# TensorE in program order through the main loop of a four-layer convolution and attention kernel, and four steps of a side chain moved

## The chip, the cores and the metric

The kernel runs on one core of one Trainium2 chip. The time is the device time of one execution in microseconds (us). Before the change it is 1875.23 us, the median of three runs (1875.23 to 1875.4).

The engines are named as in the profile: PE is TensorE's matmul, PEld its weight load, DVE is VectorE, ACT is ScalarE, POOL is GpSimd, SP is SyncE, which issues most transfers. A float32 matmul appears as two records, two passes, each with its own weight load.

## What is computed

The input is 8 batches of 512 channels by 32 x 32 positions (N = 1024), all in float32. Four layers follow each other.

```python
# layer 0: attention without softmax, divided by its largest singular value
f = relu(batchnorm(Wf x)); g = relu(batchnorm(Wg x)); h = Wh x      # 64 channels
z = f^T g; x = Wv (h (z / sigma_max(z))^T) + x
# layer 1: group norm, then softmax attention with 512 channels
hn = groupnorm(x); q, k, v = Wq hn, Wk hn, Wv hn
x = x + Wp (softmax(q^T k / sqrt(512)) v)
# layer 2: softmax attention with 128 channels
t, p, g = split(W_w x); x = batchnorm(Z_w (softmax(t^T p / sqrt(128)) g)) + x
# layer 3: a 1x1 convolution of signs
s = bn(scale * (sign(W) sign(x + bias))) + x; out = where(t > 0, t, slope * t) + bias2   # t = s - shift
```

The largest singular value is found by repeated squaring of a small matrix, in a chain of 64 x 64 products per pair of batches (`chain`), with the matrix turned by VectorE between two products.

## The kernel before

The work before the main loop (to about 175 us of the span) does layer 0's projections for all batches, the merged weights of layer 1, and the singular value of the first pair of batches. The main loop then calls `fast(env, n, hb, ua)` for n = 0 to 7, one batch each. One call traces, in this order:

1. `scores1`: layer 1's logits and their exponentials, four groups of seven products (Strassen-like, `seven`, L422). Each of `seven`'s results is copied by ScalarE (`move`, L367) or added by VectorE (`plus`, L373). The matmuls are called by the names of their factors: A11·B11, S1·T1, S2·T2, S4·B22, S3·T3, A12·B21, A22·T4, in that order. A11·B11, S2·T2, S3·T3 and A22·T4 go into one bank of PSUM, S1·T1 and S4·B22 into a second, A12·B21 into a third. Between two of these steps the last half of layer 3 of the batch before (`leave`, held in `rest3`) is traced, and the entry of the next batch: `weights0` (L313) and `enter` (L446, L467, L474), matmuls with 64 rows or a few columns.
2. `make_v` (values of layer 1), with the sums of exponentials (L1033, `inverse_sums`) and their way through memory.
3. `values1` (L751), which ends layer 1. In it the next batch is normalized, and the first two factors for its U are prepared (`prepare_u`, on POOL, L582 to L584, with a load of `fac` by SP).
4. `project2`: layer 2's projections, seven products (L422) and then 8 steps of 4 matmuls (L852).
5. `scores2`: 8 x 2 logits (L1011), each with its exp on ScalarE (L1018); VectorE adds the exponentials (L1005).
6. `values2` (L1172), `inverse_sums` (L1033), `close2` (L871), the first half of layer 3 (`leave`: signs L882 on ScalarE, products L894, then L905, L906, L907, L915, L937, L938, L945 on ScalarE and VectorE).

U of the next batch (`make_u2`) is made in the gaps of stages 4 and 5: a generator of 7 x 4 steps, of which `fill()` takes one after each step of `project2` (15) and after each L1011 (16). One block of four steps is `inner`: seven small products (L606, 128 x 256, 0.43 us each in two passes) into two banks. `p1` holds two of the sums, `pa` in its left half and `pc` in its right half; `p2` holds the third, `pb`.

```python
product(pa, 0, True, False);  move(d11, pa)      # step 0
product(pc, 3, False, False); move(d22, pc)
product(pa, 2, False, False); move(d12, pa)      # step 1
product(pc, 4, False, True);  plus(d12, pc, d12, 0)
product(pa, 5, False, False); plus(d22, pa, d22, 1)   # step 2
product(pb, 1, True, True);   plus(d11, pb, d11, 0)
product(pa, 6, False, True);  move(d21, pa, 1)   # step 3
```

`move` is a copy by ScalarE (L623, or L625 with a bias), `plus` an addition by VectorE (L617, or L619 with a bias). At the end of a block POOL adds finished parts into U by transfers (L658), and the next factors are prepared.

The chain for the singular values of the other pairs of batches runs behind all this: `chore(now)` takes one step of it. In batch 0 there are 23 such places: 10 in `scores1`, 4 in `make_v`, 5 in `values1` and 4 in `project2`. A step is one or two L1239 and perhaps an L1276 on PE, with copies by ScalarE (L1257) or VectorE (L1259, L1261), turns by VectorE (L1246, L1251), sums of a diagonal (L1270), and at a chain's start a power on POOL (L1289). At the end of a chain ScalarE takes a logarithm (L1318) and an exponential (L1321), each with a load of its table, VectorE scales in between (L1319 to L1323).

The order in which each engine gets its instructions is set by a scheduler while the program is built: it goes by a model of times and by priority, so it may take an instruction ahead of one that was traced earlier if that one would still wait. Exceptions are instructions marked with `keep_in_program_order`, and blocks under `manual_schedule`, in which the named engine's instructions keep the order in which they were traced. Before the change the work ahead of the main loop has such a block for PE, and the main loop has none. The scheduler adds all waits that data or a shared bank need.

## Time and profile before

| what | time |
|---|---|
| median of three runs | 1875.23 us |
| profiled execution | 1877.21 us, of which span 1875.3 us |
| PE busy | 1851.4 us |
| DVE busy | 1181.0 us |
| ACT busy | 572.2 us |
| POOL busy | 379.5 us |

The span is the time from the first to the last instruction of the profiled execution; its own time is 1.9 us longer. TensorE's granted clock was 0.998 of full speed.

Batch 1, cut at the first matmuls of its stages (us from the span's start; each row is how long an engine was busy in that stretch):

| stretch | stage | length | PE | DVE | ACT | POOL |
|---|---|---|---|---|---|---|
| 498.2 to 547.1 | `values1` | 48.9 | 48.90 | 39.40 | 3.93 | 20.66 |
| 547.1 to 580.6 | `project2` with U | 33.5 | 33.39 | 18.00 | 8.38 | 13.42 |
| 580.6 to 604.1 | `scores2` with U | 23.5 | 23.50 | 10.57 | 12.72 | 12.37 |
| 604.1 to 616.5 | `values2` | 12.4 | 12.40 | 9.89 | 0.96 | 0.86 |
| 616.5 to 627.6 | `close2` and first half of `leave` | 11.1 | 11.10 | 6.76 | 5.35 | 0.00 |
| 627.6 to 709.9 | next batch's `scores1`, `make_v` | 82.3 | 82.29 | 59.09 | 34.88 | 1.18 |

How to read the profile's lines: a line of the timeline has the start in us, the length in us, the engine, the line of the kernel, the operation, what it writes and reads, the shape and how many instructions are merged into it, and in brackets how long the engine was idle before it and what released it. A line of the waits has the engine and what waited, what it waited for, the total in us, how often, and the longest.

### The profile page before, as it was taken

How to read it: one execution, taken by the hardware profiler on the slowest of the kernel's cores; microseconds unless marked ns; L12 is line 12 of the kernel's file. 1: busy time of each engine (PE TensorE's matmuls, PEld its weight loads, DVE VectorE, ACT ScalarE, POOL GpSimd, SP SyncE). 2: the span in 40 equal slices, each digit the busy share in tenths (PEclk: the TensorE clock that was granted, in tenths of full speed). 3: DMA queues.
4: the chain of work that ended last, by engine and by line, in shares of the span. 5: the costliest groups of instructions: out<-in, count | busy, mean ns of one | idle time of the engine just before them, and what ended most of it. 6: DMA issues, size and time to landing. Idle time of an engine off the chain costs nothing.

```text
span 1875.3 us, 18038 instructions
## 1 busy us (share of the span) xinstructions
PE 1851.4 (99%) x6490; PEld 1004.1 (54%) x6490; DVE 1181.0 (63%) x2188; ACT 572.2 (31%) x1022; POOL 379.5 (20%) x403
## 2 busy tenths in 40 slices
PE   9999999999999999999999999999999999999997
PEld 3365464644646465654646455654646464644653
DVE  3356777567765768567764777467654767366447
ACT  2042221344213521244214522244213521244114
POOL 1002004310224003420224003320234004310011
PEclk9999999999999999999999999999999999999999
DMA  8641000242006210242006210242006200340001
GB/s 280 202 137 46 20 17 1 65 101 89 12 10 128 92 37 1 56 105 85 21 4 125 84 54 1 52 108 80 21 10 128 97 25 1 71 91 23 12 1 47
DMA packets 57532, 119.05 MB, mean 63 GB/s; under 512 B 7200, under 2 KB 17244, under 8 KB 57180
## 3 DMA queue, kind: packets, MB, share of 16 engines
q1 hardware_dynamic: 42844, 91.70, 14.8%
q0 software_dynamic: 13728, 25.70, 8.0%
q8 instruction: 53, 0.87, 0.2%
q10 hardware_dynamic: 864, 0.43, 0.1%
q14 instruction: 43, 0.35, 0.1%
HBM read 68.92 MB, written 23.20 MB: 49 GB/s over the span
## 4 chain that ended last, share of the span: by engine, by line
PE 95%; DVE 3%; ACT 1%; DMA 1%; issue 0%; POOL 0%; DVEq 0%; ACTq 0%
PE bank L422 37%; PE bank L751 21%; PE bank L606 8%; PE bank L1172 6%; PE bank L1011 5%; PE bank L1560 4%; PE bank L871 3%; PE bank L852 3%; PE bank L446 2%; PE bank L894 1%; PE wide L1606 1%; PE bank L1664 1%; PE bank L1239 1%; PE quad L1452 0%; PE bank L1033 0%; DVE st L458 0%
## 5 line engine op out<-in xcount | busy, mean ns | idle before, releaser
L751 PE MATMUL bank<-e,vt 128*128 128x512 f32 x768 | 336.2, 594 | 0.0
L751 PEld LDWEIGHTS bank<-e,vt 128*128 128x128 f32 x768 | 144.3, 190 | 172.3 <-issue 167.2
L422 PE MATMUL bank<-ut,h 128*128 128x512 f32 x384 | 180.7, 597 | 0.0
L244 POOL TENSOR_TENSOR r_r<-r_v,minus_half 128x4 f32<-128x4 f32 (+1 forms) x11 | 11.0, 1001 | 699.6 <-DVE r_v L243 694.2
L1011 PE MATMUL bank<-tpg 128*128 128x512 f32 x256 | 126.6, 592 | 0.0
L606 PE MATMUL bank<-jit,fac 128*128 128x256 f32 x392 | 118.5, 390 | 4.4 <-ACT ut L623 2.4
L422 PEld LDWEIGHTS bank<-ut,h 128*128 128x128 f32 x384 | 71.2, 190 | 90.7 <-issue 79.2
L422 PE MATMUL bank<-us,hs 128*128 128x512 f32 x256 | 118.9, 597 | 0.1
L1172 PE MATMUL bank<-e,tpg 128*128 128x512 f32 x256 | 114.7, 595 | 0.0
L606 PEld LDWEIGHTS bank<-jit,fac 128*128 128x128 f32 x392 | 67.3, 189 | 76.6 <-issue 24.9
L373 DVE TENSOR_TENSOR e<-bank,e 128x512 f32<-128x512 f32 x96 | 65.8, 689 | 61.9 <-PE bank L422 55.8
L1018 ACT ACTIVATE e<-bank 128x512 f32<-128x512 f32 x128 | 76.4, 597 | 87.0 <-PE bank L1011 87.0
L582 POOL TENSOR_TENSOR jit<-h 128x256 f32<-128x256 f32 x56 | 49.5, 905 | 209.7 <-PE bank L606 122.8
L422 PE MATMUL bank<-wo,h 128*128 128x256 f32 x384 | 89.8, 384 | 0.0
L367 ACT COPY e<-bank 128x512 f32<-128x512 f32 x96 | 55.0, 581 | 95.1 <-PE bank L422 88.7
L422 PEld LDWEIGHTS bank<-us,hs 128*128 128x128 f32 x256 | 47.6, 190 | 63.1 <-issue 54.8
L1172 PEld LDWEIGHTS bank<-e,tpg 128*128 128x128 f32 x256 | 48.1, 190 | 57.4 <-issue 56.9
L422 PEld LDWEIGHTS bank<-wo,h 128*128 128x128 f32 x384 | 71.4, 190 | 12.6 <-issue 3.8
L882 ACT ACTIVATE sg<-xt,rb 128x512 f16<-128x512 f32 x64 | 44.2, 717 | 106.5 <-DVE xt L873 103.7
L623 ACT COPY ut<-bank 128x256 f32<-128x256 f32 x126 | 46.9, 372 | 96.2 <-PE bank L606 93.4
L373 DVE TENSOR_TENSOR vt<-bank,vt 128x512 f32<-128x512 f32 x48 | 33.2, 692 | 66.3 <-PE bank L422 65.5
L367 ACT COPY vt<-bank 128x512 f32<-128x512 f32 x64 | 37.4, 584 | 121.3 <-PE bank L422 121.2
(391 smaller groups left out, 3341.0 us busy)
## 6 DMA issues: line engine op xcount, KB each, us to landing
xt<-in_x SPq DMA_DIRECT2D x55, 512.0 KB
fac<-fac_dram SPq DMA_DIRECT2D x49, 448.0 KB
out<-both SPq DMA_DIRECT2D x63, 256.0 KB
ut<-ut POOLq DMA_DIRECT2D x28, 512.0 KB, 5.0
ut<-p POOLq DMA_DIRECT2D x42, 256.0 KB, 4.1
rfull<-r_dram SPq DMA_DIRECT2D x15, 512.0 KB
f_dram<-f SPq DMA_DIRECT2D x8, 256.0 KB
fb<-f_dram SPq DMA_DIRECT2D x8, 256.0 KB
```

What stands on the lines that cost most here:

```text
L367: nc.scalar.copy(dst, ps)
L373: nc.vector.tensor_tensor(dst, ps, u, ALU.add)
L422: mm(out=ps[:, q * w : (q + 1) * w], lhsT=lt(ka, kb, q, k), rhs=rhs(ka, kb, q, k), start=first and q == 0 and k == 0, stop=last and k == 1 ...
L582: tt(t[:, k], b[:, k, hi], b[:, 0, bass.ts(k, QF)], ALU.subtract)
L606: mm(out=out, lhsT=fac[:, blocks[a], :], rhs=rhs[b], start=first, stop=last, skip_group_check=True,)
L751: mm(out=ps, lhsT=a[:, t, bass.ts(r_, P)], rhs=e[t], start=first and t == 0, stop=last and t == NTH - 1, skip_group_check=True,)
L852: mm(out=ps[:, i, :], lhsT=xt[:, cc, bass.ts(4 * h + i, P)], rhs=sbw["tpg"][:, cc, 2 * P : 3 * P], start=cc == 0, stop=cc == CC - 1,)
L871: mm(out=ps, lhsT=sbw["z"][:, bass.ts(oc, P)], rhs=att, start=True, stop=True)
L1011: mm(out=ps, lhsT=pt[:, 0, bass.ts(t, P)], rhs=tt[:, 0, half(h)], start=True, stop=True,)
L1018: nc.scalar.activation(e[:, half(h)], ps, AF.Exp, scale=float(P) ** -0.5)
L1172: mm(out=banks[h], lhsT=gt[:, t, :], rhs=es[t][:, half(h)], start=t == 0, stop=t == NT - 1,)
L1560: mm(out=banks[i][side(h), :], lhsT=w0[i][:, cc, :], rhs=xt[:, cc, half(h)], start=cc == 0, stop=cc == CC - 1,)
```

## The change

The calls of `fast` in the main loop are traced in a `manual_schedule` block for PE. So TensorE's instructions of the main loop stand in the program in the order in which the code traces them; the other engines are still ordered by the scheduler. And in batch 0 (n == 0) the four `chore` steps that were taken in `project2`, after its steps 2, 5, 8 and 12, are taken in `scores2`, after the second half of t = 1, 3, 5 and 7. In the batches after it nothing is moved by hand.

```diff
         for k, _ in enumerate(project2(env, xt, made)):
             fill()
-            chore(k in (2, 5, 8, 12))
+            chore(n and k in (2, 5, 8, 12))
         tt, pt, gt = made
 
         def between(t, h):
             fill()
+            chore(n == 0 and h and t in (1, 3, 5, 7))
 
         es, esum = scores2(env, pt, tt, between)
@@
         ua = got[0]
         late_u = factors_of_u(env)
-        for n in range(B):
-            hb, ua = fast(env, n, hb, ua)
+        with tc.manual_schedule(engines={mybir.EngineType.PE}):
+            for n in range(B):
+                hb, ua = fast(env, n, hb, ua)
```

In the built programs, two parts of TensorE's order in batch 1 (L606 with the number of the product in `inner`):

```
        before                            after
scores2, sixth block of U (and the fifth's last product)
        L1011                             L1011
        L606 5 (fifth block)              L606 6 (fifth block)
        L606 0                            L1011
        L1011                             L606 0
        L606 6 (fifth block)              L606 3
        L606 3                            L1011
        L1011                             L606 2
        L606 2                            L606 4
        L606 1                            L1011
        L1011                             L606 5
        L606 4                            L606 1
from the end of scores2 to the next batch's scores1
        L1011 x2, L606 6, L1172 x3        L606 6, L1011 x3, L1172 x2
        L1033 x4                          L1033 x4
        L1172 x10, L871 x4, L1172 x3      L1172 x10, L871 x4, L1172 x4
        L894 x8, L871 x4                  L894 x8, L871 x4
        A11 B11 x2, S1 T1 x2              A11 B11 x2, S1 T1 x2
        L894, half of A12 B21             S2 T2 x2
        S2 T2 x2                          S4 B22 x2
        L894 x2, half of A12 B21          L894 x4
        S4 B22 x2, L894, S3 T3 x2         S3 T3 x2, A12 B21 x2
        L894 x4, A22 T4 x2                L894 x4, A22 T4 x2
```

Elsewhere in the loop the order differs in the same way in `project2`; in `scores1` of batches 1, 3 and 5 the two L313 stand together after the change and apart before it, in batches 2, 4 and 6 the four L446 of the first visit. In `make_v` and `values1` nothing moves. SP's order is the same, and POOL's differs only in the place of L1289.

## The prediction

> **What bounds the kernel now.** I read the page first: busy shares, then the chain that ended last.

> ```profile
> PE 1851.4 (99%) x6490; PEld 1004.1 (54%) x6490; DVE 1181.0 (63%) x2188; ACT 572.2 (31%) x1022; POOL 379.5 (20%) x403
> ...
> PE 95%; DVE 3%; ACT 1%; DMA 1%; issue 0%; POOL 0%; DVEq 0%; ACTq 0%
> ```

> TensorE (PE) is the bound: it stands still for 1875.3 − 1851.4 = 23.9 us in all, so nothing can be gained beyond that and some packing, while any wait put into its queue is added to the end. The list of waits, for PE alone, has almost nothing on the line that makes U (L606):

> ```profile
> PE bank L606 <- ACT ut L623: 2.4, 2, 2.0
> ```

> The timeline of batch 0 shows why:

> ```profile
> 333.53 0.59 PE L606 MATMUL bank<-h,fac 128*128 128x256 f32 x2
> ...
> 333.96 1.02 PE L422 MATMUL bank<-xd,sp 128*128 128x512 f32 x2
> 334.21 0.38 ACT L623 COPY ut<-bank 128x256 f32<-128x256 f32 x1
> ...
> 334.64 0.37 PEld L606 LDWEIGHTS bank<-jit,fac 128*128 128x128 f32 x2 [0.49 <-ACT ut L623]
> 334.82 0.59 PE L606 MATMUL bank<-jit,fac 128*128 128x256 f32 x2
> ```

> A product of `inner` ends, ScalarE copies it out, and the weights of the next L606 wait for that copy, since `pa` and `pc` are halves of one bank (`p1`). One L422 (0.86 us) lies between and covers it. Timelines at the seam between two batches and at the end of `scores2` come below.

> [...]

> **Part 1: pairs of L606.** `inner` issues products 0,3 | 2,4 | 5,1 | 6. In program order nothing stands inside a step, so 3 follows 0 and 4 follows 2 directly, each waiting for the copy of its partner; 1 goes to another bank and is free. The trace of before has no such pair; its price from parts: from the start of the first product to its last record's end 0.59, to the copy 0.04, the copy 0.37, to the next weight load 0.05, and 0.11 until it streams. That last one is from a stall in the same timeline, where the next matmul comes 0.54 after this one instead of 0.43:

> ```profile
> 349.88 0.70 PE L606 MATMUL bank<-jit,fac 128*128 128x256 f32 x2 [0.47 <-DVE ut L617]
> ...
> 350.42 0.59 PE L606 MATMUL bank<-hs,fac 128*128 128x256 f32 x2
> ```

> That makes 1.16 us instead of 0.43: a stall of 0.73 with ScalarE free. Less is excluded, as every part is needed. Behind L1011 the exp (L1018, 0.60 us, beginning 0.20 after L1011's end) runs until 0.80, so the copy starts 0.17 later: 0.90. More than 0.90 needs another instruction in ScalarE's queue; I take 0.73 and 0.90. Per batch seven blocks of U, two pairs each: in `scores2` 6 pairs at 0.90, in `project2` 2 at 0.90 (behind L367, 0.59 us) and 6 at 0.73. That is 5.4 + 1.8 + 4.4 = 11.6 us, and 7 batches make U (98 such pairs stand in the new order, none in the old): **+81.1**.
> What goes: the present stalls of these two stages, by starts beyond the streaming time: 0.64 + 2.12 + 0.17 + 0.47 = 3.4 in batch 0 and about 1.2 in each of the six later ones (0.83 + 0.42 in batch 4): **−10.6**. Between steps stand L422 x2 (1.72), L852 x4 (0.88) or L1011 (0.86), over the 0.73 needed, so 2 after 3 and 5 after 4 cost nothing as long as ScalarE and VectorE are free.

> **Part 2: the seam between batches.** In the timeline of batch 1:

> ```profile
> 627.64 1.88 PE L422 MATMUL bank<-ut,h 128*128 128x512 f32 x4
> ...
> 629.36 1.88 PE L422 MATMUL bank<-us,hs 128*128 128x512 f32 x4
> ...
> 631.70 0.56 ACT L367 COPY e<-bank 128x512 f32<-128x512 f32 x1
> ...
> 632.32 1.98 PE L422 MATMUL bank<-us,hs 128*128 128x512 f32 x4
> ...
> 634.72 1.05 ACT L367 COPY e<-bank 128x512 f32<-128x512 f32 x2
> ...
> 635.43 1.90 PE L422 MATMUL bank<-us,h 128*128 128x512 f32 x4
> ```

> S2·T2 (632.32) waits for the copy of A11·B11 (ends 632.26), S4·B22 (635.43) for that of S1·T1 (ends 635.25). The copies stand behind L937, L938 and L882 of `leave`. Before, L894s and half of A12·B21 fill the room; in the new order S2·T2 and S4·B22 follow at once, and L1172 x4 instead of x3 stands before the first L894, which moves that ScalarE work 0.86 later. Counted from the first L871 (616.47): S1·T1 ends at 3.43 + 3.43 + 1.72 + 3.43 + 3.43 = 15.45; the copy ends at 15.79 + 0.86, plus 0.16 to the stream, 16.8: stall 1.35. S2·T2 ends at 18.5, the second copy allows 19.8: stall 1.28. Waits of 0.34 here go: net 2.3, seven times: **+16.1**. If the work of `leave` does not move, 1.7 of each goes.

> **Part 3: L1033.** Only two L1172 (1.72 us) precede it, not three:

> ```profile
> 603.24 3.88 DVE L1005 TENSOR_TENSOR esum<-esum,e 128x1024 f32<-128x1024 f32 x3
> ...
> 604.55 2.74 PE L1172 MATMUL bank<-e,tpg 128*128 128x512 f32 x6
> ```

> The sum ends at 607.12, just when the third L1172 does. In the new order exp (0.20 + 0.60) and the last add (1.23) follow the last L1011, with handoffs 2.2 us against 1.72: 0.5 for batches 1 to 6, 0.3 in the last (the same on L1062): 3.3.
> Batch 0 is worse: the four chores, the same instructions (on PE L1239 and L1276, 0.11 us a pass), now end a chain inside `scores2`, where VectorE was busy 14.4 of 28 us. Its two table loads (1.28 each), L1318 and L1321 stand on ScalarE before three of the exps, and on VectorE (DVE) three adds wait for `rsig` and then queue with the next chain's 2.3 us. I count from the start of L1011 for t = 6: exp free at 1.7; rsig 5.1; gm 5.7; two adds 8.2; chain 10.4; last add 11.7, while PE arrives at 6.0: 5.7. Together **+9.0**. In exchange POOL's pow (L1289) no longer stands before `jit` work; what it cost is among the 3.4. DMA issues: SP's order is unchanged, POOL's additions (L658) keep theirs, and later matmuls give them more room.

> **Part 4: packing.** Matmuls of 64 rows run side by side when adjacent:

> ```profile
> 652.32 1.12 PE L446 MATMUL bank<-fb,pv 64*128 64x512 f32 x2
> ...
> 655.29 1.98 PE L446 MATMUL bank<-fb,pv 64*128 64x512 f32 x6
> ```

> One alone holds PE 1.05, three 1.91; four together take 1.92 elsewhere. Three such quads (batches 2, 4, 6) and three split pairs of L313 (batches 1, 3, 5) are whole in the new order: 6 × 1.05 = **−6.3**.

> Sum: 81.1 + 16.1 + 9.0 − 10.6 − 6.3 = **+89.3**. The profiled execution took 1877.2 (span 1875.3 and 1.9 around it), the median 1875.2; the same amount goes on both. Forecast for the median: **1964 us**.

> **Rivals.** (a) Bank waits only: the seam is covered, all pairs cost 0.73: 98 × 0.73 + 9.0 − 16.9 = +64, 1939 us. For: the waits of `leave` are estimates from one batch; against: the copies already end last there. (b) Evictions queue: the gap between steps has some 0.1 us to spare, and an add (1.23) ahead of L617 or an exp ahead of L623 costs another 0.5 per pair: +49, 2013 us. [...] against: with PE slower it is idle half the time. (c) Faster: if a pair's wait cost under 0.17 us and the seam nothing, parts 1 and 4 would win: at 0.1, 9.8 − 16.9, 1868 us. The point is the turnaround PE, ScalarE, PE; the measured parts give 0.73. (d) The new order changes nothing PE notices: 1875; against it the new order itself, in which the pairs are adjacent.

> **How the numbers follow.** Forecast 0.66, with its own range 1948 to 1985; (a) 0.17, (b) 0.12, (c) 0.03, (d) 0.02. The range 1930 to 1995 leaves out (c), (d) and most of (b). A measurement tells about 0.2% (3.8 us) from no change: faster 0.03, same 0.02, slower 0.95.

> **What would show it.** PE's waits list L606 after ACT L623 some 80 to 98 times, 0.6 to 0.8 idle each; L422 after ACT L367 about 1.3 twice per seam; L1033 after DVE L1005 once of some 5 us; L313 and L446 only in full groups. No L606 wait in the list would make the prediction wrong; L606 waiting for DVE would be rival (b).

## The result and the profile after

The changed kernel takes 1960.86 us (median of five runs, 1960.32 to 1961.92); the kernel before, run beside it, 1875.23 us. The ratio is 1.0456 with a 95% interval of 1.0441 to 1.0472: slower by 4.6%, 85.6 us. The profiled execution has a span of 1958.7 us, 83.4 more than the 1875.3 of before.

In the changed kernel the first 1163 lines of the code are where they were; a line after them is one further down (L1172 is L1173 here).

The page of the changed kernel, busy times and instructions by engine:

```profile
PE 1863.8 (95%) x6490; PEld 996.4 (51%) x6490; DVE 1177.3 (60%) x2188; ACT 569.5 (29%) x1022; POOL 378.8 (19%) x403
```

The instructions are the same in number on every engine. TensorE's busy time grew by only 12 us, while 1958.7 − 1863.8 = 94.9 us of the span are now idle, against 23.9 before. No other engine has become the bound: all are at most 60% busy. So the question is only what TensorE waits for. Its list of waits (what waited, for what, us in total, how often, the longest):

```profile
PE bank L606 <- ACT ut L623: 35.8, 70, 0.6
PE bank L422 <- ACT e L367: 16.2, 18, 1.1
PE bank L606 <- ACT p L623: 15.8, 28, 0.6
PE bank L1033 <- DVE esum L1005: 7.1, 7, 5.7
```

Four rows hold 74.9 of the 94.9 us. The first and the third are the pairs of L606: 70 + 28 = 98 waits, 14 in each of the seven batches that make U. The second is the seam between batches. The fourth is one wait of 5.7 us in batch 0 and six of 0.2 to 0.3.

One pair in the timeline of the changed kernel (batch 4, `scores2`; start, length, engine, line, what; in brackets the idle time before and its releaser):

```profile
1270.44 0.59 PE L606 MATMUL bank<-hs,fac 128*128 128x256 f32 x2
...
1270.64 0.60 ACT L1018 ACTIVATE e<-bank 128x512 f32<-128x512 f32 x1 [0.33 <-PE bank L1011]
1271.14 0.37 ACT L623 COPY ut<-bank 128x256 f32<-128x256 f32 x1
...
1271.62 0.30 PEld L606 LDWEIGHTS bank<-jit,fac 128*128 128x128 f32 x2 [0.98 <-POOL jit L582]
1271.65 0.67 PE L606 MATMUL bank<-jit,fac 128*128 128x256 f32 x2 [0.61 <-ACT ut L623]
...
1272.15 1.02 PE L1011 MATMUL bank<-tpg 128*128 128x512 f32 x2
```

Product 0 of a block streams from 1270.44. Its copy L623 waits until the exp L1018 is out of ScalarE's way and runs from 1271.14; product 3 starts only at 1271.65, and the L1011 behind it waits with it. From one L606 to the next are 1.21 us instead of 0.43.

### The profile page after: what moved, and what is told of

Its sections match the earlier page's. It is cut to its first block, busy times and chain, and to the rows that moved or that the text cites. A ratio compares the mean times of both kernels' runs of the same rounds, so it can differ in the third digit from the quotient of the medians.

```text
span 1958.7 us, 18010 instructions
## 1 busy us (share of the span) xinstructions
PE 1863.8 (95%) x6490; PEld 996.4 (51%) x6490; DVE 1177.3 (60%) x2188; ACT 569.5 (29%) x1022; POOL 378.8 (19%) x403
## 5 line engine op out<-in xcount | busy, mean ns | idle before, releaser
L422 PE MATMUL bank<-ut,h 128*128 128x512 f32 x384 | 178.1, 598 | 1.4 <-ACT e L367 1.4
L606 PE MATMUL bank<-jit,fac 128*128 128x256 f32 x392 | 120.8, 390 | 27.4 <-ACT ut L623 18.9
L1011 PE MATMUL bank<-tpg 128*128 128x512 f32 x256 | 126.2, 593 | 0.0
L422 PE MATMUL bank<-us,hs 128*128 128x512 f32 x256 | 117.5, 596 | 7.6 <-ACT e L367 7.6
L422 PEld LDWEIGHTS bank<-ut,h 128*128 128x128 f32 x384 | 70.9, 190 | 95.1 <-issue 84.3
L1173 PE MATMUL bank<-e,tpg 128*128 128x512 f32 x256 | 115.9, 600 | 0.0
L606 PEld LDWEIGHTS bank<-jit,fac 128*128 128x128 f32 x392 | 66.2, 189 | 97.3 <-issue 45.8
L1018 ACT ACTIVATE e<-bank 128x512 f32<-128x512 f32 x128 | 76.2, 597 | 117.1 <-PE bank L1011 117.1
L582 POOL TENSOR_TENSOR jit<-h 128x256 f32<-128x256 f32 x56 | 49.8, 909 | 233.1 <-PE bank L606 146.1
L422 PE MATMUL bank<-wo,h 128*128 128x256 f32 x384 | 89.9, 384 | 0.0
L367 ACT COPY e<-bank 128x512 f32<-128x512 f32 x96 | 55.1, 581 | 102.2 <-PE bank L422 102.2
L422 PEld LDWEIGHTS bank<-us,hs 128*128 128x128 f32 x256 | 47.8, 190 | 69.8 <-issue 56.2
L617 DVE TENSOR_TENSOR ut<-bank,ut 128x256 f32<-128x256 f32 x63 | 26.8, 425 | 89.9 <-PE bank L606 89.8
L1173 PEld LDWEIGHTS bank<-e,tpg 128*128 128x128 f32 x256 | 48.5, 192 | 61.0 <-issue 60.9
L623 ACT COPY ut<-bank 128x256 f32<-128x256 f32 x126 | 46.9, 372 | 108.3 <-PE bank L606 108.3
L422 PEld LDWEIGHTS bank<-wo,h 128*128 128x128 f32 x384 | 71.4, 190 | 12.6 <-issue 3.8
L882 ACT ACTIVATE sg<-xt,rb 128x512 f16<-128x512 f32 x64 | 44.1, 715 | 107.2 <-DVE xt L873 104.4
```

Of the source, the lines that this page charges most:

```text
L367: nc.scalar.copy(dst, ps)
L422: mm(out=ps[:, q * w : (q + 1) * w], lhsT=lt(ka, kb, q, k), rhs=rhs(ka, kb, q, k), start=first and q == 0 and k == 0, stop=last and k == 1 ...
L582: tt(t[:, k], b[:, k, hi], b[:, 0, bass.ts(k, QF)], ALU.subtract)
L606: mm(out=out, lhsT=fac[:, blocks[a], :], rhs=rhs[b], start=first, stop=last, skip_group_check=True,)
L617: nc.vector.tensor_tensor(dst, ps, t, ALU.add)
L623: nc.scalar.copy(dst, ps)
```

## The experiments

The theory: the two adjacent L606 of a step share bank `p1`, so each second one waits for the copy of the first, and these 98 waits make most of the loss; the seam and the moved chores make the rest. The rivals: program order costs as such, whatever the banks are, and the waits move on when they are taken away; or the moved chores carry a good part. All times are medians; each ratio is against the kernel before on the same chip.

| kernel | us | ratio to before, 95% interval |
|---|---|---|
| changed kernel | 1960.9 | 1.0456 (1.0441 to 1.0472) |
| order alone | 1955.8 | 1.0426 (1.0408 to 1.0443) |
| chores alone | 1874.5 | 0.9988 (0.9981 to 0.9995) |
| changed, `pc` in `p2` | 1883.8 | 1.0037 (1.0023 to 1.0051) |
| changed, A12·B21 early | 1953.3 | 1.0408 (1.0391 to 1.0426) |
| before, `pc` in `p2` | 1867.4 | 0.9952 (0.9938 to 0.9966) |
| order, `pc` in `p2`, A12·B21 early | 1872.8 | 0.9980 (0.9973 to 0.9987) |
| the same, chores at t = 1 to 4 | 1872.0 | 0.9978 (0.9970 to 0.9987) |
| chores alone, `pc` in `p2` | 1869.5 | 0.9965 (0.9951 to 0.9978) |
| changed, `values2` cut as before | 1958.2 | 1.0437 (1.0420 to 1.0455) |
| order, `pc` in `p2`, early, cut | 1870.6 | 0.9969 (0.9957 to 0.9982) |
| the same, one chore at t = 2 | 1870.9 | 0.9967 (0.9955 to 0.9980) |

**The two halves of the change.** First the order without the chores, then the chores without the order. Against the kernel before:

```diff
 # order alone
-        for n in range(B):
-            hb, ua = fast(env, n, hb, ua)
+        with tc.manual_schedule(engines={mybir.EngineType.PE}):
+            for n in range(B):
+                hb, ua = fast(env, n, hb, ua)
 # chores alone
-            chore(k in (2, 5, 8, 12))
+            chore(n and k in (2, 5, 8, 12))
...
+            chore(n == 0 and h and t in (1, 3, 5, 7))
```

> Program order for TensorE in the main loop, the four chores left in project2. Theory (pair waits, seam): all of the loss is the order's; against the changed kernel only the batch-0 stall of L1033 (5.7 us) and the lowered clock after it (about 2 us) go, and some 2 us of waits in project2 come back, so about 1955, 5 us under the changed kernel. If the moved chores carried a substantial part of the loss (rival): under 1945.

> The scheduler orders TensorE as before, the four chores moved to scores2 of batch 0. Theory: it can put other matmuls over the wait of L1033, so within 4 us of 1875 either way. Rival (the moved chores cost by themselves): the 5.7 us and the lowered clock show here too, 1881 to 1885.

Both came as the theory had them: 1955.8 and 1874.5. The order alone makes 4.3% of the 4.6%. In its waits L1033 has no long one any more:

```profile
PE bank L1033 <- DVE esum L1005: 1.6, 7, 0.2
```

The same chores in the same place under the scheduler's order cost nothing (0.12% faster, less than the 0.2% that tells a change from none). Its timeline shows what the scheduler did:

```profile
388.99 4.54 PE L1173 MATMUL bank<-e,tpg 128*128 128x512 f32 x10
394.03 0.64 PE L1033 MATMUL bank<-esum,ones 128*32 128x256 f32 x8 [0.50 <-DVE half__3033 L1293]
```

It put ten passes of L1173 (five matmuls) ahead of L1033 in batch 0, where the code traces two matmuls there, so VectorE's late sum met 4.3 us of work and 0.5 us of idle time was left. So the moved chores cost about 5 us only together with the fixed order.

**The shared bank.** In the changed kernel `pc` goes to the left half of `p2`, and `pb` to the right half; the sums and their copies are the same.

```diff
-        pa, pc, pb = p1[:, lo], p1[:, hi], p2[:, lo]
+        pa, pc, pb = p1[:, lo], p2[:, lo], p2[:, hi]
...
-        product(pc, 3, False, False)
+        product(pc, 3, True, False)
...
-        product(pb, 1, True, True)
+        product(pb, 1, False, True)
```

> Changed kernel with pc in the left half of p2 instead of the right half of p1, so that products 0, 3 and 2, 4 of inner lie in different banks. Theory: the 98 waits of L606 for L623 are 98 x 0.62 to 0.77, about 65 us, and go: 1896, the list of waits shows no or few L606. In the new layout 5 and 1 of step 2 are in p1 and p2 too. Rival (program order costs by itself, the waits move to the next product in the same bank): 1940 or more.

It took 1883.8 us: 77 of the 85.6 us are gone, in program order, with no instruction less. The two rows of L606 have left the list of waits, and the seam's row stays as it was:

```profile
PE bank L422 <- ACT e L367: 16.4, 18, 1.2
PE bank L1033 <- DVE half__3035 L1293: 5.7, 1, 5.7
```

Its timeline in the same stage of batch 4 has the pair back to back, 0.43 us apart (1225.08 and 1225.51), with the exp beside it:

```profile
1225.08 0.59 PE L606 MATMUL bank<-jit,fac 128*128 128x256 f32 x2
...
1225.28 0.60 ACT L1018 ACTIVATE e<-bank 128x512 f32<-128x512 f32 x1 [0.86 <-PE bank L1011]
...
1225.51 0.59 PE L606 MATMUL bank<-hs,fac 128*128 128x256 f32 x2
...
1225.94 1.02 PE L1011 MATMUL bank<-tpg 128*128 128x512 f32 x2
```

The rival that program order costs by itself is out as the main cause; some 7 us above the kernel before are left (1883.8 against 1876.5 on the same chip). My expectation was 12 us too high: I had counted only what a pair loses until the second product's first pass. The second pass loses some too, because its weights come late as well: their load starts 0.08 us (at 1271.65) or 0.11 us (at 565.82) after the first pass has begun in the changed kernel's trace, and with it in a product that didn't wait (0.08 to 0.10 us lost, starts counted against 0.21 a pass). By stage lengths the edit gives 6.07 us per batch in `project2` and 4.6 to 4.9 in `scores2`, 76.2 us in all, or 0.78 us a pair.

Is it the bank or the order, then? The same edit on the kernel before:

> The bank edit alone on the kernel before (pc into p2, the scheduler orders TensorE). Theory: the shared bank costs the kernel before only what its interleaving doesn't cover, 0.37 per batch in project2 and 0.4 in scores2 (its rows against those of the changed kernel with the bank edit), so 5 us less at most: 1869 to 1873. Rival (the bank edit saves about as much here as in the changed kernel, 77 us, so the order isn't what made it matter): under 1810.

1867.4 us, a gain of 8.6, a little more than expected, against 77 in the changed kernel. So the shared bank costs much only where the order puts its two users side by side: the scheduler's interleaving had hidden nearly all of it.

But this kernel no longer has that interleaving. With the bank free, the scheduler puts the two products of a step side by side, as the code traces them. In its timeline products 0 and 3 of a block stand together (batch 5, `scores2`):

```profile
1418.82 0.59 PE L606 MATMUL bank<-hs,fac 128*128 128x256 f32 x2
1419.25 0.59 PE L606 MATMUL bank<-jit,fac 128*128 128x256 f32 x2
1419.68 1.02 PE L1011 MATMUL bank<-tpg 128*128 128x512 f32 x2
```

In `project2` and `scores2` of all eight batches its trace has the lines of TensorE's instructions in the same order as program order with the chores left in place; in the other stages, from `values1` of batch 0 on, it has the order of the kernel before. So in these two stages the scheduler had left program order because of the shared bank, and the 8.6 us are the bank edit and the new order together; the bank edit under the old interleaving, held fixed, was not run. The waits on L606 are down to two, both in batch 0's `project2`, where the chores stand:

```profile
PE bank L606 <- DVE ut L619: 1.8, 1, 1.8
...
PE bank L606 <- ACT ut L623: 0.9, 1, 0.9
```

This is the fastest kernel of the study, faster than the kernel before and the changed one.

**The seam.** In the changed kernel, A12·B21 of the first group of `scores1` is traced right behind A11·B11, ahead of S1·T1. `seven` has an option for that, `early`. (Lines are one further down again in this kernel: L894 is L895.)

```diff
-                term, lo[:, half(0)], hi[:, half(0)], lo[:, half(1)], hi[:, half(1)], exp=scale
+                term, lo[:, half(0)], hi[:, half(0)], lo[:, half(1)], hi[:, half(1)], exp=scale,
+                early=i == 0,
```

> Changed kernel with A12 B21 of the first group of scores1 traced right after A11 B11 (into the third bank), before S1 T1. Theory: 1.72 us of work stands between A11 B11 and S2 T2, so the first stall of the seam (1.25, seven times) goes and the second (1.2) becomes smaller or stays: 9 to 17 us less, 1944 to 1952. Rival (the copies stay as far behind since all of ScalarE's queue of leave moves along): 1958 to 1961.

The seam of the changed kernel first, in its timeline of batch 1:

```profile
652.74 1.88 PE L422 MATMUL bank<-ut,h 128*128 128x512 f32 x4
...
654.46 1.88 PE L422 MATMUL bank<-us,hs 128*128 128x512 f32 x4
...
656.80 0.56 ACT L367 COPY e<-bank 128x512 f32<-128x512 f32 x1
...
657.42 1.98 PE L422 MATMUL bank<-us,hs 128*128 128x512 f32 x4 [1.08 <-ACT e L367]
...
659.82 1.05 ACT L367 COPY e<-bank 128x512 f32<-128x512 f32 x2
660.44 1.98 PE L422 MATMUL bank<-us,h 128*128 128x512 f32 x4 [1.04 <-ACT e L367]
```

S2·T2 (657.42) and S4·B22 (660.44) each wait for a copy that starts only when ScalarE is done with the work of `leave`. With the edit the time is 1953.3, 7.5 less; the theory's sign was right and its size too large. The timeline of that kernel:

```profile
653.27 3.60 PE L422 MATMUL bank<-ut,h 128*128 128x512 f32 x8
656.71 3.60 PE L422 MATMUL bank<-us,hs 128*128 128x512 f32 x8
660.14 1.03 PE L895 MATMUL bank<-sg,sw 128*128 128x512 f16 x4
661.00 1.96 PE L422 MATMUL bank<-us,h 128*128 128x512 f32 x4
662.80 1.88 PE L422 MATMUL bank<-ut,h 128*128 128x512 f32 x4
...
664.21 1.40 DVE L916 SCALAR_TENSOR_TENSOR both<-both,sa,xt 128x512 f32<-128x512 f32 x2
665.53 0.68 DVE L373 TENSOR_TENSOR e<-bank,e 128x512 f32<-128x512 f32 x1
666.27 1.98 PE L422 MATMUL bank<-ut,hs 128*128 128x512 f32 x4 [0.73 <-DVE e L373]
```

Both old waits are gone: the four passes of A12·B21 (among the eight at 653.27) cover the first copy, and with it the second is early enough. But A12·B21 had stood between S3·T3 and A22·T4, which share a bank, and is now missing there: A22·T4 (666.27) waits 0.73 us for the addition that takes S3·T3's sum (662.80) out of the bank, and that addition stands behind `leave`'s own L916 on VectorE. The cover was moved from one wait to another, smaller one. By stage lengths the seven seams became 9.2 us shorter, which is within the forecast; but the edit also reaches `scores1` of batch 0, which has no seam, and there A22·T4 waits 1.3 us in the same way.

The prediction had the extra L1172 ahead of the first L894 make ScalarE's work 0.86 us later. I read that as a part of the seam's price that could be had back, and cut `values2` in the changed kernel as the kernel before has it:

```diff
-        values2(0, range(0, 2))
+        values2(0, range(0, 3 if more else 2))
...
-            values2(0, range(2, NTH))
+            values2(0, range(3, NTH))
...
-            values2(1, range(0, NTH))
+            values2(1, range(0, NTH + 1))
...
-            att = values2(1, range(NTH, NT))
+            att = values2(1, range(NTH + 1, NT))
```

> Changed kernel with its matmuls of values2 cut as the kernel before had them: three L1172 ahead of the four L1033 instead of two, eleven after the first close instead of ten, so three instead of four ahead of the first L894. Theory: L1033 waits nothing (0.25 less, six times), the ScalarE work of leave moves 0.86 ahead of the seam, and the two stalls at S2 T2 and S4 B22 fall from 1.25 and 1.20 to some 0.4 each: 1.5 + 7 x 1.7 = 13 less, 1948. Rival (the copies are held by something that doesn't move with the L894, as VectorE's part of leave): only L1033 gains, 1959.

It took 1958.2, near the rival's number, and the timeline has the same two waits to the hundredth:

```profile
650.41 1.33 ACT L937 ACTIVATE up<-both,cb 128x512 f32<-128x512 f32 x2 [1.35 <-DVE both L915]
...
651.54 1.88 PE L422 MATMUL bank<-ut,h 128*128 128x512 f32 x4
...
656.22 1.99 PE L422 MATMUL bank<-us,hs 128*128 128x512 f32 x4 [1.08 <-ACT e L367]
...
659.24 1.98 PE L422 MATMUL bank<-us,h 128*128 128x512 f32 x4 [1.04 <-ACT e L367]
```

But the rival's reason is not it either. The L1172 stands ahead of the L894, and so ahead of the second L871 and of A11·B11 as well: take it away, and ScalarE's chain and TensorE's arrival both come earlier by the same amount. A11·B11 starts 1.13 us after L937 here and in the changed kernel (1.13 = 652.74 − 651.61 there, 651.54 − 650.41 here). The place of the L1172 is no term of the seam at all. What was gained is L1033's: by stage lengths 0.3 in each of six batches, where the third L1172 covers the wait. In batch 0 the wait is 4.8 us instead of 5.7, but the matmuls after it run at half clock for some 5.5 us instead of 3.4 (see the last section), and nothing is left of that. Another 1.1 us of the difference between the two traces lies ahead of the first `values1`, where TensorE's order is the same in both, and is no gain of the edit.

**Versions put together.** These ask whether the parts add up, and whether program order can beat the scheduler once its waits are mended.

> Program order, bank edit, A12 B21 early in the first group of scores1, and the chores left in project2. If the parts add up: 1883.8 - 7.6 for the seam - 5.1 for the chores = 1871, below the kernel before. If project2 then waits for the chores' table loads (2.2 in the run with the order alone) without the bank waits to hide them: up to 1875.

1872.8, 2 us above the sum of the parts. As foreseen, `project2` of batch 0 waits for the chores: 36.50 us against 31.47 in the kernel whose chores have left, with the same two waits on L606 as above, 1.8 and 0.9 us. With the bank waits around them it had been 4.4 (41.97 against 37.54). In the kernel before, with the chores in the same place, each of their table loads takes 1.28 us on ScalarE, and an L606 waits 1.96 us for a copy behind two of them; the power takes 1.00 us on POOL, with VectorE idle for 1.05 us until it ends.

> As the previous kernel, but the four chores in scores2 of batch 0, after the second halves of t = 1, 2, 3 and 4 instead of 1, 3, 5 and 7. Theory: the chain then ends some 10 us of TensorE time earlier, VectorE has caught up with the sums by the end, and L1033 waits 0.3 as in the other batches, with no lowered clock: 1867 to 1870. If VectorE's queue still ends late, L1033 waits 2 to 5 us: 1871 to 1876.

1872.0, a miss. The long wait on L1033 is gone (0.2 us at most are left), its clock drop too (a mean granted clock of 0.999 against 0.997 in the changed kernel), but the chores cost their time earlier: `scores2` of batch 0 takes 27.60 us against 23.28 in the other batches. The waits in that kernel that replace it:

```profile
PE bank L606 <- DVE p L619: 1.1, 1, 1.1
...
PE bank L606 <- DVE p L617: 0.8, 1, 0.8
```

The U products wait for VectorE, whose queue is held by the chain: ahead of the L617 at 377.64 stand five sums from 376.23 on, ahead of the L619 at 386.34 the turns from 384.44 to 385.83 and three small instructions that follow the power. The four chore steps cost 5.0 us in `project2` and 4.3 in the middle of `scores2`; in the changed kernel, towards the end of `scores2`, they cost 8.4 (0.9 in that stage and 7.5 in `values2`, against batch 2). Under a fixed order no place among these is free.

> Bank edit and moved chores with the scheduler's order of TensorE. If the parts add up (1874.5 for the chores alone, 0.75 per batch for the banks): 1868 to 1871; if the scheduler's choices shift, up to 1876.

1869.5, inside the range written down. But the parts don't add up: with the 8.6 us that the bank edit had given alone, the sum would be 1865.9. In the trace the scheduler put eight passes of L1173 ahead of L1033 instead of ten, and L1033 now waits 4.0 us in batch 0. With the bank edit the moved chores cost 2.1 us under the scheduler's order (1869.5 against 1867.4). That they are free there holds for one balance of the times, not in general.

> Bank edit, program order, A12 B21 early and the cut of values2 together, chores in project2. The seam's remaining stalls (1.3 per batch on VectorE's sum, from the same leave) shrink by up to 0.86, L1033 by 0.25: between 1864 and 1869, if the parts add up; 1872 if the seam now hangs on VectorE.

> As the previous kernel, with the last of the four chores after t = 2 of scores2 and three in project2. The stall of 2.0 that the power on POOL makes in project2 goes, some 0.5 to 1.3 come in scores2: 1 to 1.5 us below the previous kernel. If VectorE stalls as long there: equal.

1870.6 and 1870.9. The first gained 2.2 where up to 9 was held possible: L1033's 0.3 in six batches, and nothing at the seam, as in the cut alone. In the second the wait in `project2` was traded for one of 2.5 us on L617 in `scores2`: equal, the second of the two outcomes written down for it. With all of this mended, program order is still some 3 us behind the scheduler's order with the same bank edit (the two intervals just overlap). In `project2` and `scores2` the kernel of 1870.6 us and that of 1867.4 us have the same order. By stage lengths the 3.5 us between their spans lie elsewhere: 1.9 ahead of the first `values1` (1.3 of it the wait of A22·T4 in batch 0), 1.2 in the last seam and 1.2 in the last batch, less 0.8 in other stages.

## Why the prediction was right

Forecast were 1964 us, measured 1960.9, by the mechanism given. The forecast's sum of +89.3 stands against +83.4 in the spans. Stages are cut at the same instructions in both traces, and what the change carries from one stage into another is set back: the last L606 product (0.43 us in each of seven batches), and the last matmuls of the moved chores (0.36 us in batch 0).

| term | forecast | measured |
|---|---|---|
| pairs of L606 | +81.1 | +76.2 |
| old stalls of `project2`, `scores2` gone | −10.6 | −13.1 |
| seam and packing | +16.1 − 6.3 = +9.8 | +9.8 |
| L1033 and batch 0 | +9.0 | +9.3 |
| last batch, and ahead of the first `values1` | not in it | +0.8 + 0.5 = +1.3 |

**Pairs.** The count of 98 is exact. The price with ScalarE free was put together as 0.73, and product 4 after 2 has it: 0.625 until the second product streams and 0.104 in its second pass. Product 3 after 0 has it too behind L422, but costs 0.72 + 0.08 = 0.80 behind L852. Behind an exp 0.90 was forecast: product 3 after 0 costs 0.77 + 0.08 = 0.85, product 4 after 2 only 0.68 + 0.10 = 0.79. The step "runs until 0.80, so the copy starts 0.17 later" took the exp's whole record. In the timeline of the pair above the exp begins at 1270.64 and the copy behind it at 1271.14, 0.10 before the exp's 0.60 us end: two ScalarE records in a row overlap, so the copy is late by 0.07. Behind L852 and L1011 product 3 starts 0.09 later after the copy's end than product 4 does; its weight load is put down to POOL's L582 there. The first two blocks, whose factors were made ahead in `values1`, don't have this loss, which fits; but whether POOL is the cause was not tried. The mean of 0.82 instead of 0.90 makes 3.5 us in `scores2`, and 0.79 behind L367 another 1.5; 0.80 instead of 0.73 for product 3 behind L852 gives 1.0 back. These prices come from starts and make 76.9 us for 98 pairs; by stage lengths, against the kernel with `pc` in `p2`, it is 76.2. In the list of waits a pair stands with 0.5 to 0.6 us of idle time, less than the 0.6 to 0.8 that were named as a sign.

**Old stalls.** The pairs' bank costs the kernel before more than its listed waits say. By stage lengths the six later batches had 0.9 to 2.2 us each (8.6 in all, 7.2 were forecast from one batch), and batch 0, from which the chores leave, 4.5 instead of 3.4.

**Seam and packing.** Forecast were 1.35 and 1.28 at S2·T2 and S4·B22; the trace has 1.25 and 1.20. Not foreseen was a third wait of 0.51 us, at S3·T3 of the second group, for another L367 copy, in the batches where no L313 pair stands in front. The seam thus cost 2.7 in the last of the seven, where nothing is packed, instead of 2.3. Packing gave some 1.3 us a batch instead of 1.05, so the two errors cancel in the sum: that this term came out exactly is luck. The reasoning that `leave` would move by 0.86 was true and empty, as the cut of `values2` showed.

**L1033.** 5.7 us were forecast in batch 0 and 5.70 came, by the queue on VectorE that the prediction named: in the changed kernel's timeline the next chain's turns stand ahead of the last sum.

```profile
403.54 0.51 DVE L1247 STREAM_TRANSPOSE gm<-cur 64x64 f32<-64x64 f32 x2
404.07 0.85 DVE L1252 STREAM_TRANSPOSE gm<-cur 32x32 f32<-32x32 f32 x4
404.96 1.23 DVE L1005 TENSOR_TENSOR esum<-esum,e 128x1024 f32<-128x1024 f32 x1
...
406.24 1.08 PE L1033 MATMUL bank<-esum,ones 128*32 128x256 f32 x8 [5.70 <-DVE esum L1005]
```

The six later batches had 0.3 instead of 0.5. What the step left out is the clock after the wait, 1.7 us (below). The last batch's 0.8 is an L894 that in program order stands behind the count of bad rows (0.8 us for L986 on VectorE), which no step looked at. The 0.5 ahead of the first `values1` is no effect of the change: TensorE's order is the same there, and the stretch is between 281.7 and 282.8 us long in the traces of the eight kernels without the A12·B21 edit.

Of the rivals, (a) is out, since the seam was not covered; (b), too: no L606 waits for VectorE in the changed kernel. (c) set its point at a pair price of 0.17, and its sum left out the 9.0 of part 3; with them the point is 0.08. Measured is 0.78, so it is out either way.

## What to carry to other kernels

In this kernel two results in halves of one bank acted as one resource, with 98 waits on L606 in program order and no such row once `pc` was in `p2`: put into different banks whatever may become adjacent, before an order is fixed (here 77 us in program order, 8.6 with the scheduler, which had ordered around the shared bank). An order fixed by hand needs, at each place where TensorE reads what another engine has just written, enough other work in front of it; read from the trace where that work stood, for one stage's queue of ScalarE or VectorE was the next one's wait here (5.70 us at L1033, 1.08 and 1.04 at the seam). Work that is moved to cover one wait is missing where it stood, as A12·B21 was (0.73 us). Before moving an instruction ahead of a wait, check that the wait's other side doesn't hang on the same instruction: what delays both moves nothing.

## What the runs showed of the hardware

```profile
400.00:404.00 4.00, 0.54 (x2) 0.00 (x0) 3.34 (x9) 0.87 (x2) 0.57 (x1) 0.85 0.40 71
404.00:406.00 2.00, 0.00 (x0) 0.00 (x0) 1.90 (x6) 0.00 (x0) 0.00 (x0) 0.50 0.00 0
406.00:408.00 2.00, 1.76 (x9) 0.70 (x10) 1.02 (x4) 0.00 (x0) 0.00 (x0) 0.50 0.00 0
408.00:410.00 2.00, 2.00 (x4) 0.85 (x3) 2.00 (x2) 0.00 (x0) 0.00 (x0) 0.58 0.00 0
410.00:412.00 2.00, 2.00 (x6) 0.81 (x6) 1.97 (x3) 0.00 (x0) 0.00 (x0) 1.00 0.09 27
```

The clock was 0.50 before TensorE took up work again at 406.24 and stayed low for about 3.4 us of it; two passes of L1173 started 0.85 us apart instead of 0.43. `values2` of this batch took 18.90 us against 11.37 in batch 2; 5.5 of the difference is the longer wait, 0.4 the last matmuls of the moved chores, and the other 1.7 the clock. The mean of 0.85 in the first stretch means that the clock fell near 402.8, 2.3 us after TensorE's last matmul; it came back 3.4 us after work began. In the changed kernel with `pc` in `p2` the wait was the same 5.7 us, to 394.66, and the clock came back only near 401.0, 6.3 us later:

```profile
398.00:400.00 2.00, 2.00 (x3) 0.68 (x2) 1.97 (x3) 0.00 (x0) 0.00 (x0) 0.50 0.01 2
400.00:402.00 2.00, 2.00 (x5) 0.91 (x4) 2.00 (x2) 0.00 (x0) 0.00 (x0) 0.76 0.69 262
402.00:404.00 2.00, 2.00 (x6) 0.80 (x6) 0.45 (x2) 0.00 (x0) 0.00 (x0) 1.00 0.01 2
```

Its `values2` of batch 0 is 1.4 us longer than the changed kernel's, which is half of the 2.9 us more at half clock. So after two waits of the same length the full clock came back after 3.4 and after 6.3 us of work; what sets that time was not shown. Every kernel here with a wait of 4.0 us or more at L1033 shows the half clock (waits of 4.0, 4.8 and 5.7 us); the waits on L606 of 1.96 us in the kernel before and of 2.5 us in the last one of the table left it at 1.00. So a single long wait of TensorE cost more than its length: half the time worked at half clock on top, 1.7 us here and 3.1 us there, after the same wait.
